# Half of the first expert weights of layer 1 loaded during the attention of its second batch element

## The chip, the cores and the metric

The kernel runs on one core of one Trainium2 chip. A core has a matrix engine (PE, with its weight loads PEld), a vector engine (DVE), a scalar engine (ACT), a general-purpose engine (POOL), and a queue that issues most transfers (SP); 16 DMA engines move the data. All of them run on their own and meet at semaphores. The metric is the device time of one execution in microseconds; lower is better. The whole computation is one launch.

## The reference

Four layers follow each other on an activation `x` of 2 batch elements, 1,024 tokens each, 256 features. Each layer adds a cross-attention over a context of 64 rows and then a second block, each scaled by the tanh of a gate. Layer 1's second block is the one that matters here (NQ = 16 query heads, NKV = 4 key heads, head size 16, 8 experts, HID = 512):

```python
h = rmsnorm(x, ln1_w)
q = rmsnorm(apply_rope(h @ Wq + bq), qn_w)
k = rmsnorm(apply_rope(h @ Wk + bk), kn_w)
v = h @ Wv + bv
...
attn = softmax(where(causal, q k^T / sqrt(HD), -inf))
out = attn v
out = out * sigmoid(out @ Wg + bg)
x = x + out @ Wo + bo
h2 = rmsnorm(x, ln2_w)
logits = h2 @ Wr + br
top1 = argmax(logits)
u = h2 W1[top1] + b1[top1]
act = u[:HID] * sigmoid(u[HID:])
return x + act W2[top1] + b2[top1]
```

Each token goes to one expert. W1 has 256 x 1,024 values for each of the 8 experts, W2 has 512 x 256.

## The kernel before

The 2,048 tokens are 16 tiles of 128 rows. Tiles 0 to 7 are the first batch element, tiles 8 to 15 the second. The self-attention is causal, so a tile attends only to itself and the tiles of its own batch element ahead of it. Memory is given out from two ends: pools on the left, and pools marked `side="right"`, which are held longer. Within PE, layer 1's instructions run in the order in which the program writes them (`manual_schedule`); the other engines' order comes from the framework's scheduler, which also adds waits where a tile takes the memory of an older one.

Stages of layer 1's second block, with what they hold:

- `l1` (L943) opens the right-hand pool `l1f`: 16 row tiles `qk0` to `qk15` (320 values a partition each; rows of q and k, later the new residual `u` in their first 256), `ln2`, the one-hot of the choice `oh`, and the buffer `hbuf` in device memory.
- `l1_front` (L966) makes q, k and v for all 16 tiles, while layer 1's cross-attention still runs. `norm` normalises, `turn` transposes four tiles into `hT` (two buffers), `qkv` multiplies and writes `v` (a tile of 16 x 4 x 32 values, all tokens) and `r` (six buffers), and `divided` turns `r` into the rows `qk`.
- `l1_attention` (L1093) goes tile by tile through the causal attention. `stack` splits a tile's q and k into high and low parts on POOL, and PE transposes them. `greatest` takes scores for the row maxima; their transpose `mT` is copied by DMA, issued by POOL, into the padded rows of `qT` (L1222). `scores` multiplies and exponentiates into `eT` (a pool with three buffers, also named `l1e`); `values` multiplies by `v` into `po`; when a tile is done, its transposes `pq` give `r` and `o` on DVE (L1271, L1273), and the transposes of `o` go into `oT` (a tile of 2 x 2,048 values, all tokens).
- For every group of four finished tiles, `routed` (L1345) queues `gate`, `out` (out-projection, writes the residual `u`), `normed` (writes the normalised rows to `hbuf` by SP, L1321), `turned` and `chosen` (logits and the choice). These are fed one by one between the scores of later tiles: `chosen` of group 1, the first batch element's last, runs while the second element's tiles are being done.
- `l1_experts` (L1564) opens the pool `l1e` with the whole of W1 (`w1`, 2 x 8,192 values a partition, 64 KB) and W2 (`w2`, 8,192 values, 32 KB). SP issues eight loads of W1 of 1 MB each (L1576) and eight of W2 of 1 MB each (L1580). They take memory that attention held, so they start when it is done. `sort_tiles` (L1441) sorts tokens by expert in the pool `l1r`; its constants (a triangular matrix `upper`, five index rows made by POOL iotas at L1427 and copied by DVE at L1429) need no data. Then up to 23 token tiles run, each with one expert: `gather` fetches rows `xg` (L1592) and biases `bt` (L1598) by indices on POOL's queue, `turn` transposes the rows (`xt`, L1609; DVE scales them into `xT`, L1611), `up` multiplies by W1 in two halves of four matmuls (L1625), `back` transposes, `down` multiplies by W2 (`y`, L1645) and scatters the rows to `ybuf`.
- Layer 2 begins with the loads of `l2_l3_xattn` (`lw`, L1815, and `cx`, L1817) and of its weights (`wi`, L1700, and nine further), all on SP, and takes `ybuf` back to `x` in `take` (L1680).

The weights as they were declared and loaded:

```python
w1 = pool.tile([P, DC, E1 * 2 * H1], F32, tag="w1", name="w1")
w2 = pool.tile([P, FC, E1 * D], F32, tag="w2", name="w2")
for e in range(E1):
    nc.sync.dma_start(
        out=w1[:, :, ts(e, 2 * H1)], in_=a["L1_ffn_W1"][e].rearrange("(k p) h -> p k h", p=P)
    )
```

Of the kernel before, what the change touches and what calls it, by code (L numbers as in the profile page):

```python
# [11 lines left out]
F32 = mybir.dt.float32  # L12
# [8 lines left out]
P = 128  # L21
B, S, D = 2, 1024, 256
T = B * S
NT = T // P
# [16 lines left out]
class Net:  # L41
# [901 lines left out]
    def l1(self, take, taken, back):  # L943

        tc = self.tc
        with tc.tile_pool(name="l1f", bufs=1, side="right") as pool:
            rows = [
                pool.tile([P, (NQ + NKV) * HD], F32, tag=f"qk{i}", name=f"qk{i}") for i in range(NT)  # L950
            ]
            ln2 = pool.tile([P, DC], F32, tag="ln2", name="ln2")
            self.nc.sync.dma_start(out=ln2, in_=self.a["L1_ffn_ln2_w"])

            u = [r[:, :D] for r in rows]
            oh = pool.tile([P, NT, E1], F32, tag="oh1", name="oh1")
            hbuf = self.dram.tile([T, D], F32, tag="hbuf", name="hbuf")
            with tc.tile_pool(name="l1a", bufs=1, side="right") as fp:
                es = ExitStack()
                f = self.l1_front(fp, es.enter_context(tc.tile_pool(name="l1q", bufs=1, side="right")), rows)  # L960
                rest = sum(self.l1_xattn(f["steps"], take), [])
                taken()
                self.l1_attention(u, f, rest, es.close, ln2, oh, hbuf)
            return self.l1_experts(ln2, oh, hbuf, back())

    def l1_front(self, keep, pool, rows):  # L966
        nc, a = self.nc, self.a
        NH = NQ + NKV
        n = NH * HD
# [15 lines left out]
        nc.gpsimd.tensor_tensor(kw, kw, kn, ALU.mult)  # L985
        nc.gpsimd.tensor_scalar(kw, kw, HD**-0.5, None, ALU.mult)

        v = keep.tile([P, NT, NKV, 32], F32, tag="v", name="v")
        pv = pool.tile([P, 32], F32, tag="pv", name="pv")
        nc.gpsimd.memset(pv, 0.0)  # L990
        nc.gpsimd.memset(pv[:, HD : HD + 1], 1.0)
# [12 lines left out]
        def padded(i):  # L1004

            kf = kT.rearrange("p h t -> p (h t)")
            if i < 8:
                nc.scalar.copy(kf[64:128, ts(i, 1024)], pk[64:128].to_broadcast([64, 1024]))
            elif i < 10:
                j = slice(8 * (i - 8), 8 * (i - 7))  # L1010
                nc.scalar.copy(
                    v[:, j].rearrange("p i k c -> p (i k) c"),
                    pv[:, None, :].to_broadcast([P, 8 * NKV, 32]),
                )

# [17 lines left out]

        def turn(i):
            if i % 4 == 3:
                hT[i // 4] = pool.tile([P, DC, 512], F32, tag="hT", name="hT", bufs=2)
                self.transposed(
                    [hn[j] for j in range(i - 3, i + 1)], hT[i // 4], 4,
                    evac=lambda o, p, c: nc.scalar.copy(o, p),
                )  # L1040

        def qkv(i):

            p = self.ps("qkv")
# [10 lines left out]
            nc.scalar.copy(  # L1055
                v[:, i, :, :HD], p[:, n:384].rearrange("p (k c) -> p k c", k=NKV)
            )
# [14 lines left out]
            nc.vector.tensor_reduce(group["ss"][:, i % 4, :], sq, AX.X, ALU.add)  # L1072
            nc.vector.tensor_tensor(r, r, t, ALU.add)
# [16 lines left out]
            off=off, ones=ones,  # L1090
        )

    def l1_attention(self, u, front, rest, front_done, ln2, oh, hbuf):  # L1093

# [5 lines left out]
        with ExitStack() as es:  # L1100
# [149 lines left out]
            def values(i, kt, eT):  # L1250
                b, qt = divmod(i, SB)
                if kt == 0:
                    state["po"] = self.psum.tile([P, 512], F32, tag="po", name="po")
                po = state["po"]
                for kv in range(NKV):
                    nc.tensor.matmul(  # L1256
                        po[32 * kv : 32 * kv + 32, :], v[:, b * SB + kt, kv, :], eT[:, kv, :],
                        start=kt == 0, stop=kt == qt,
                    )
                if kt < qt:  # L1260
                    return []
                pT = state["pool"].tile([P, 512], F32, tag="pT", name="pT", bufs=2)
                nc.scalar.copy(pT, po)

                def turn():
                    t = self.ps("pq")
                    for j in range(4):
                        nc.tensor.transpose(t[:, ts(j, P)], pT[:, ts(j, P)], self.ident)
                    t = t.rearrange("p (j k c) -> p k j c", j=4, k=NKV)
                    r = ap.tile([P, NKV, 4], F32, tag="r", name="r", bufs=2)  # L1270
                    nc.vector.reciprocal(r, t[:, :, :, HD])  # L1271
                    o = ap.tile([P, D], F32, tag="o", name="o", bufs=2)
                    nc.vector.tensor_tensor(  # L1273
                        o.rearrange("p (k j c) -> p k j c", k=NKV, j=4), t[:, :, :, :HD],
                        r[:, :, :, None].to_broadcast([P, NKV, 4, HD]), ALU.mult,
                    )
                    state["o"] = o

                def back():
                    t = self.ps("ot")  # L1280
                    for c in range(DC):
                        nc.tensor.transpose(t[:, ts(c, P)], state["o"][:, ts(c, P)], self.ident)
                    nc.scalar.copy(oT[:, :, ts(i, P)], t[:, :D].rearrange("p (c q) -> p c q", c=DC))

                routing.extend(routed(i))
                return [turn, back]
# [2 lines left out]

            def gate(g, c):  # L1290
                p = self.ps("gate")
                o = oT[:, c, ts(g, 512)]
# [5 lines left out]
            def out(i):  # L1298
                p = self.ps("wo")
                nc.tensor.matmul(p[:, :D], ones, borow, start=True, stop=False)  # L1300
                for c in range(DC):
                    nc.tensor.matmul(
                        p[:, :D], oT[:, c, ts(i, P)], wo[:, c, :], start=False, stop=c == DC - 1
                    )

                y = ap.tile([P, D], F32, tag="y", name="y", bufs=2)
# [26 lines left out]
            def chosen(g):  # L1333
# [227 lines left out]
        nc.vector.tensor_copy(sca, row)  # L1561
        return gat, sca, ia

    def l1_experts(self, ln2, oh, hbuf, way):  # L1564
        nc, tc, a = self.nc, self.tc, self.a
        FC = H1 // P
        NS = NT + E1 - 1
# [1 line left out]
        with ExitStack() as es:  # L1569
            pool = es.enter_context(tc.tile_pool(name="l1e", bufs=1, reuse_waits="tile"))  # L1570
            gi, si, ei = (pool.tile([P, NS], I32, tag=n, name=n) for n in ("gi", "si", "ei"))
            used = pool.tile([P, 1], I32, tag="used", name="used")
            w1 = pool.tile([P, DC, E1 * 2 * H1], F32, tag="w1", name="w1")
            w2 = pool.tile([P, FC, E1 * D], F32, tag="w2", name="w2")
            for e in range(E1):
                nc.sync.dma_start(  # L1576
                    out=w1[:, :, ts(e, 2 * H1)], in_=a["L1_ffn_W1"][e].rearrange("(k p) h -> p k h", p=P)
                )
            for e in range(E1):
                nc.sync.dma_start(  # L1580
                    out=w2[:, :, ts(e, D)], in_=a["L1_ffn_W2"][e].rearrange("(k p) d -> p k d", p=P)
# [34 lines left out]
            def up(s, w):  # L1616
# [6 lines left out]
                p, u, h = ups[s], ub[s], slice(w * H1, (w + 1) * H1)  # L1623
                for k in range(DC):
                    nc.tensor.matmul(  # L1625
                        p[:, h], xT[s][:, k, :], w1[:, k, bass.ds(reg[s] * (2 * H1) + w * H1, H1)],
                        start=k == 0, stop=k == DC - 1,
                    )
                nc.vector.tensor_tensor(u[:, h], p[:, h], bt[:, h], ALU.add)  # L1629
# [733 lines left out]
```

## Time and profile before

| | us |
|---|---|
| timed runs | 2134.15, 2143.36, 2151.75 |
| their median | 2143.36 |
| the profiled execution's own time | 2131.65 |
| its span, first to last instruction | 2129.8 |

The profiled execution is one run, a little below the three timed ones; durations below are its own. PE was granted 0.922 of its full clock over the span. Over the span the engines were busy as follows: PE 1832.9 us (86%), PEld 1161.1 (55%), DVE 1130.2 (53%), ACT 839.8 (39%), POOL 416.3 (20%).

The stretches in which layer 1's second block lies, in that execution (times from the start of the span):

| stretch, us | what runs | PE busy | PE clock | GB/s moved |
|---|---|---|---|---|
| 594 to 985 | attention, out-projection, routing | 350.3 of 391 | 0.97 | 6 |
| 985 to 1005 | tail of the routing | 13.0 of 20 | 0.82 | 27 |
| 1005 to 1050 | weights loaded, sort, first token tile | 15.2 of 45 | 0.58 | 358 |
| 1050 to 1165 | the experts | 107.8 of 115 | 1.00 | 120 |
| 1165 to 1185 | change to layer 2 | 6.2 of 20 | 0.66 | 189 |

A busy share is an average over stages with different limits, so a change in one stage is read in that stage. A line of the timeline has the start, the length, the engine, the line of the kernel, the operation, output and inputs, how many instructions were joined (x), and in brackets how long the engine had been idle before and what ended that. The chain of waits goes back from the last instruction to what released each step. A stretch with a DMA share near 1 has all 16 DMA engines taken.

### The profile page before, as it was taken

The page shows a single profiled execution, that of the slowest core. Times are in us where ns is not written, and L with a number is a line of the kernel's source. Part 1 is how long each engine was busy: PE and PEld are TensorE (multiplying, and loading weights), DVE is VectorE, ACT ScalarE, POOL GpSimd, SP SyncE. Part 2 cuts the span into 40 slices and gives each one's busy share as a digit, 9 for nine tenths or more (in the row PEclk, how much of TensorE's full clock was granted, in tenths as well). Part 3 has the DMA queues.
Part 4 walks back from the last instruction along what each step waited for, and adds up shares of the span by engine and source line. Part 5 has one row for each costly group of instructions (what it writes and reads, how often), then busy time and mean ns, then how long its engine had stood idle before and what let it go on. Part 6 is the DMA issues. An engine that isn't in the chain of part 4 may idle for free.

```text
span 2129.8 us, 26730 instructions
## 1 busy us (share of the span) xinstructions
PE 1832.9 (86%) x9860; PEld 1161.1 (55%) x9883; DVE 1130.2 (53%) x2485; ACT 839.8 (39%) x1603; POOL 416.3 (20%) x644
## 2 busy tenths in 40 slices
PE   7858999599778899897598697799999999998894
PEld 3435777466544455544254465455555655656573
DVE  5660100376677737752343776456556555665644
ACT  3402222354534474465011465544444444442131
POOL 1004222111421121023342134100000000000273
PEclk8968999899889999998799896999999999997997
DMA  4033323310000000001742320000000000002135
GB/s 148 21 104 94 116 78 113 90 32 1 7 2 2 1 12 2 2 11 55 291 151 91 104 71 1 1 1 1 1 1 1 1 1 1 1 1 89 38 102 173
DMA packets 70605, 107.12 MB, mean 50 GB/s; under 512 B 13779, under 2 KB 55382, under 8 KB 70214
## 3 DMA queue, kind: packets, MB, share of 16 engines
q1 hardware_dynamic: 54582, 63.17, 9.1%
q0 software_dynamic: 13824, 40.55, 5.7%
q8 instruction: 83, 1.36, 0.3%
q10 hardware_dynamic: 2064, 1.62, 0.2%
q14 instruction: 52, 0.43, 0.1%
HBM read 80.90 MB, written 24.15 MB: 49 GB/s over the span
## 4 chain that ended last, share of the span: by engine, by line
PE 45%; DVE 14%; ACT 7%; issue 6%; POOL 4%; DMA 3%; SPq 1%; ACTq 0%; POOLq 0%; DVEq 0%
PE s L1940 6%; PE et L1962 4%; DVE nm L1947 3%; PE s L1186 3%; PE po L1256 3%; PE sT L1237 3%; PE po L1974 3%; PE h L2130 3%; DVE nm L1192 2%; PE prj L204 2%; ACT e L1949 2%; PE po L352 2%; DMA ybuf<-yo,si 2%; DVE x L236 1%; PE s L554 1%
## 5 line engine op out<-in xcount | busy, mean ns | idle before, releaser
L1949 ACT ACTIVATE e<-s,nm 128x1024 f32<-128x1024 f32 x128 | 141.4, 1110 | 239.7 <-DVE nm L1948 207.6
L1192 DVE TENSOR_REDUCE nm<-s 128x1 f32<-128x512 f32 (+3 forms) x304 | 184.2, 657 | 68.6 <-PE s L1191 46.9
L1947 DVE TENSOR_REDUCE nm<-s 128x1 f32<-128x1024 f32 x128 | 150.4, 1217 | 88.6 <-PE s L1940 88.6
L1245 ACT ACTIVATE eT<-sT 128x512 f32<-128x512 f32 x288 | 148.8, 603 | 112.8 <-PE sT L1237 81.6
L1962 PE MATMUL et<-ident,e 128*128 128x128 f32 x1024 | 143.1, 280 | 22.0 <-ACT qT L219 6.2
L1962 PEld LDWEIGHTS et<-ident,e 128*128 128x128 f32 x1024 | 110.9, 141 | 60.7 <-DVE x L236 11.0
L1186 PE MATMUL s<-kT,qT 128*128 128x512 f32 (+3 forms) x384 | 129.6, 418 | 16.2 <-ACT qT L114 9.7
L1940 PE MATMUL s<-kT,qT 64*128 64x512 f32 x512 | 131.7, 619 | 0.0
L1974 PE MATMUL po<-eT,v 128*64 128x256 f32 x1024 | 124.7, 386 | 0.0
L112 DVE COPY eT<-et 128x512 f32<-128x512 f32 x128 | 87.8, 687 | 58.5 <-PE et L1962 58.3
L1988 POOL TENSOR_TENSOR scs<-scs,nm 128x1024 f32<-128x1024 f32 x8 | 15.2, 1903 | 527.6 <-DVE nm L1948 527.6
L1186 PEld LDWEIGHTS s<-kT,qT 128*128 128x128 f32 x384 | 73.0, 196 | 81.1 <-DVE nm L1192 26.8
L790 PE MATMUL h<-xeT,w 128*128 128x384 f32 (+1 forms) x416 | 109.4, 422 | 0.6 <-DVEq L843 0.3
L800 DVE TENSOR_TENSOR y<-yp,b 128x256 f32<-128x256 f32 (+1 forms) x34 | 14.4, 423 | 177.8 <-PE yp L808 177.2
L794 ACT ACTIVATE hT<-h,b 128x384 f32<-128x384 f32 (+1 forms) x104 | 52.9, 508 | 137.5 <-PE h L790 134.4
L808 PE MATMUL yp<-w,hT 128*128 128x256 f32 x464 | 102.8, 381 | 0.0
L1974 PEld LDWEIGHTS po<-eT,v 128*64 128x64 f32 x1024 | 68.2, 136 | 60.2 <-issue 29.1
L1237 PE MATMUL sT<-qT,kT 128*128 128x512 f32 x288 | 98.0, 455 | 1.8 <-DMA qT<-mT 1.8
L808 PEld LDWEIGHTS yp<-w,hT 128*128 128x128 f32 x464 | 88.0, 190 | 15.3 <-issue 2.1
L114 ACT COPY eT<-et 128x512 f32<-128x512 f32 x128 | 74.0, 592 | 49.5 <-PE et L1962 49.4
L790 PEld LDWEIGHTS h<-xeT,w 128*128 128x128 f32 x416 | 70.8, 192 | 35.6 <-issue 4.0
L1625 PE MATMUL up<-w,xT 128*128 x152 | 77.2, 632 | 14.5 <-DVE ub L1629 7.0
(494 smaller groups left out, 3580.5 us busy)
## 6 DMA issues: line engine op xcount, KB each, us to landing
w<-in_L_ffn_W_dram SPq DMA_DIRECT2D x24, 1024.0 KB, 6.9
y<-ybuf SPq DMA_DIRECT2D x20, 512.0 KB, 5.1
ybuf<-zero POOLq DMA_DIRECT2D x8, 512.0 KB, 7.0
hbuf<-xn SPq DMA_DIRECT2D x32, 128.0 KB, 1.8
w<-in_L_ffn_W_dram SPq DMA_DIRECT2D x8, 512.0 KB, 10.5
x<-in_x_dram SPq DMA_DIRECT2D x16, 128.0 KB, 3.4
hbuf<-hn SPq DMA_DIRECT2D x16, 128.0 KB, 1.7
L_ffn_w1T<-in_L_ffn_w1T_dram SPq DMA_DIRECT2D x1, 2048.0 KB, 7.6
```

The costliest lines, as they stand in the source:

```text
L112: self.nc.vector.tensor_copy(out, in_)
L790: nc.tensor.matmul(p[:, :m], W[e][0][:, k, ts(hc, P)], X[e][:, k, r : r + m], start=k == 0, stop=k == DC - 1,)
L808: nc.tensor.matmul(p[:m, :D], hT[:, hc, r : r + m], W[e][1][:, hc, :], start=hc == 0, stop=hc == HC - 1,)
L1186: nc.tensor.matmul(o, qT[:, h0 + j, :], kT[:, (h0 + j) // 4, b * S + k0 : b * S + k0 + m], start=True, stop=k0 + m < n,)
L1192: nc.vector.tensor_reduce(nm[:, u, h0 : h0 + nh], s[:, : nh * m].rearrange("p (h k) -> p h k", h=nh), AX.X, ALU.max, negate=True,)
L1237: nc.tensor.matmul(s, kT[:, kv, b * S + kt * P : b * S + (kt + 1) * P], qT[:, 4 * kv : 4 * kv + 4, :], start=True, stop=kt < qt,)
L1245: nc.scalar.activation(eT[:, kv, :], s, AF.Exp)
L1940: nc.tensor.matmul(s[h][:, ts(u, 512)], q["qT"][r, 0, ts(t, P)], q["kT"][r, 0, ts(u, 512)], start=True, stop=True,)
L1947: nc.vector.tensor_reduce(m, s[h], AX.X, ALU.max, negate=True)
L1949: nc.scalar.activation(e[n][h], s[h], AF.Exp, bias=m, accum_out=q["rs"][:, t, h : h + 1])
L1962: nc.tensor.transpose(p[:, ts(j, P)], e[n][h][:, ts(k + j, P)], self.ident)
L1974: nc.tensor.matmul(po[j][64 * h : 64 * h + 64, :256], grp[g]["v"][:, k, ts(h, D3X)], eT[j][h][:, k, :], start=k == 0, stop=k == KM - 1,)
```

## The change

One tile `wa` of 8,192 values a partition (32 KB) is opened in the right-hand pool. Until the first batch element is through, it stands in for tiles that had places of their own: `v` and `oT` of the first element (0 to 1,024 and 1,024 to 3,072; the second element has tiles of its own size), the two `hT` buffers of the projections (1,024 to 3,072, ahead of `oT`), the rows `qk0` to `qk7` (3,072 to 5,632) and the ring of six `r` (5,632 to 7,552). When `chosen` of group 1 has been fed, eight loads on SP write the first 128 of the 256 rows of every expert's W1 (0.5 MB each) into `wa`; each waits for what stood in its part. At the start of the experts only the second 128 rows of every W1 are loaded (eight loads of 0.5 MB, in place of the eight of 1 MB), into a tile of half the size; W2 is loaded as before. The up matmuls take their two terms from the two tiles. The number and order of matmuls are as before.

```diff
         with tc.tile_pool(name="l1f", bufs=1, side="right") as pool:
+            wa = pool.tile([P, E1 * 2 * H1], F32, tag="wa", name="wa")
+            n = (NQ + NKV) * HD
             rows = [
-                pool.tile([P, (NQ + NKV) * HD], F32, tag=f"qk{i}", name=f"qk{i}") for i in range(NT)
+                wa[:, 3072 + i * n : 3072 + (i + 1) * n] if i < SB
+                else pool.tile([P, n], F32, tag=f"qk{i}", name=f"qk{i}")
+                for i in range(NT)
             ]
...
-        v = keep.tile([P, NT, NKV, 32], F32, tag="v", name="v")
+        v = [
+            wa[:, 0:1024].rearrange("p (i k c) -> p i k c", k=NKV, c=32),
+            keep.tile([P, SB, NKV, 32], F32, tag="v", name="v"),
+        ]
...
-                hT[i // 4] = pool.tile([P, DC, 512], F32, tag="hT", name="hT", bufs=2)
+                f = 1024 + i // 4 % 2 * 1024
+                hT[i // 4] = wa[:, f : f + 1024].rearrange("p (c t) -> p c t", c=DC)
...
-            r = group[i] = pool.tile([P, NH, HD], F32, tag="r", name="r", bufs=6)
+            f = 5632 + i % 6 * n
+            r = group[i] = wa[:, f : f + n].rearrange("p (h c) -> p h c", c=HD)
...
-            oT = pool.tile([P, DC, T], F32, tag="oT", name="oT")
+            oT = [
+                wa[:, 1024:3072].rearrange("p (c t) -> p c t", c=DC),
+                pool.tile([P, DC, S], F32, tag="oT", name="oT"),
+            ]
...
                 self.first_max(ap, lb, rev, oh[:, 4 * g : 4 * g + 4, :])
+                if g == SB // 4 - 1:
+                    load()
+
+            def load():
+
+                for e in range(E1):
+                    nc.sync.dma_start(out=wa[:, ts(e, 2 * H1)], in_=a["L1_ffn_W1"][e, :P, :])
...
-            w1 = pool.tile([P, DC, E1 * 2 * H1], F32, tag="w1", name="w1")
+            w1 = [wa, pool.tile([P, E1 * 2 * H1], F32, tag="w1", name="w1")]
...
-                nc.sync.dma_start(
-                    out=w1[:, :, ts(e, 2 * H1)], in_=a["L1_ffn_W1"][e].rearrange("(k p) h -> p k h", p=P)
-                )
+                nc.sync.dma_start(out=w1[1][:, ts(e, 2 * H1)], in_=a["L1_ffn_W1"][e, P:, :])
...
-                        p[:, h], xT[s][:, k, :], w1[:, k, bass.ds(reg[s] * (2 * H1) + w * H1, H1)],
+                        p[:, h], xT[s][:, k, :], w1[k][:, bass.ds(reg[s] * (2 * H1) + w * H1, H1)],
```

The other edits index `v` and `oT` by batch element in `values`, `back`, `gate` and `out`, and pass `wa` through `l1`, `l1_front`, `l1_attention` and `l1_experts`.

More of the change, by code (lines that the diff above doesn't have):

```diff
@@ L959, in l1, with l1_front @@
                 es = ExitStack()
-                f = self.l1_front(fp, es.enter_context(tc.tile_pool(name="l1q", bufs=1, side="right")), rows)
+                f = self.l1_front(fp, es.enter_context(tc.tile_pool(name="l1q", bufs=1, side="right")), rows, wa)
                 rest = sum(self.l1_xattn(f["steps"], take), [])
                 taken()
-                self.l1_attention(u, f, rest, es.close, ln2, oh, hbuf)
-            return self.l1_experts(ln2, oh, hbuf, back())
-    def l1_front(self, keep, pool, rows):
+                self.l1_attention(u, f, rest, es.close, ln2, oh, hbuf, wa)
+            return self.l1_experts(ln2, oh, hbuf, wa, back())
+    def l1_front(self, keep, pool, rows, wa):
         nc, a = self.nc, self.a
@@ L1009, in padded @@
             elif i < 10:
-                j = slice(8 * (i - 8), 8 * (i - 7))
                 nc.scalar.copy(
-                    v[:, j].rearrange("p i k c -> p (i k) c"),
+                    v[i - 8].rearrange("p i k c -> p (i k) c"),
                     pv[:, None, :].to_broadcast([P, 8 * NKV, 32]),
@@ L1055, in qkv @@
             nc.scalar.copy(
-                v[:, i, :, :HD], p[:, n:384].rearrange("p (k c) -> p k c", k=NKV)
+                v[i // SB][:, i % SB, :, :HD], p[:, n:384].rearrange("p (k c) -> p k c", k=NKV)
             )
@@ L1091, in l1_front, with l1_attention @@
         )
-    def l1_attention(self, u, front, rest, front_done, ln2, oh, hbuf):
+    def l1_attention(self, u, front, rest, front_done, ln2, oh, hbuf, wa):
         nc, tc, a = self.nc, self.tc, self.a
@@ L1256, in values @@
                     nc.tensor.matmul(
-                        po[32 * kv : 32 * kv + 32, :], v[:, b * SB + kt, kv, :], eT[:, kv, :],
+                        po[32 * kv : 32 * kv + 32, :], v[b][:, kt, kv, :], eT[:, kv, :],
                         start=kt == 0, stop=kt == qt,
@@ L1282, in back @@
                         nc.tensor.transpose(t[:, ts(c, P)], state["o"][:, ts(c, P)], self.ident)
-                    nc.scalar.copy(oT[:, :, ts(i, P)], t[:, :D].rearrange("p (c q) -> p c q", c=DC))
+                    nc.scalar.copy(oT[i // SB][:, :, ts(i % SB, P)], t[:, :D].rearrange("p (c q) -> p c q", c=DC))
                 routing.extend(routed(i))
@@ L1291, in gate @@
                 p = self.ps("gate")
-                o = oT[:, c, ts(g, 512)]
+                o = oT[g // 2][:, c, ts(g % 2, 512)]
                 nc.tensor.matmul(p, wgbd, o, start=True, stop=True)
@@ L1302, in out @@
                     nc.tensor.matmul(
-                        p[:, :D], oT[:, c, ts(i, P)], wo[:, c, :], start=False, stop=c == DC - 1
+                        p[:, :D], oT[i // SB][:, c, ts(i % SB, P)], wo[:, c, :], start=False, stop=c == DC - 1
                     )
@@ L1562, in place, with l1_experts @@
         return gat, sca, ia
-    def l1_experts(self, ln2, oh, hbuf, way):
+    def l1_experts(self, ln2, oh, hbuf, wa, way):
         nc, tc, a = self.nc, self.tc, self.a
```

## The prediction

> **What bounds the kernel now.** The page says PE, 86% busy. An edit that moves weight loads is decided where PE is not busy, so I went from the table by stretches (five microseconds each) to the one place where the DMA engines are full, the start of layer 1's experts. Columns: stretch, length, busy time and count of PE, PEld, DVE, ACT, POOL; then granted clock, DMA share, GB/s.
> ```profile
> 995.00:1005.00 10.00, 6.16 (x24) 4.98 (x24) 0.62 (x4) 1.36 (x4) 8.59 (x14) 0.65 0.16 53
> 1010.00:1015.00 5.00, 0.00 (x0) 0.00 (x0) 5.00 (x25) 0.00 (x0) 0.00 (x0) 0.50 1.02 416
> 1035.00:1040.00 5.00, 4.22 (x6) 1.34 (x5) 0.69 (x1) 1.91 (x2) 0.00 (x0) 0.50 1.06 365
> 1045.00:1050.00 5.00, 2.20 (x6) 0.96 (x6) 1.75 (x4) 0.99 (x2) 0.94 (x1) 1.00 0.78 245
> 1060.00:1080.00 20.00, 18.96 (x71) 11.27 (x70) 8.24 (x16) 3.34 (x6) 9.70 (x10) 1.00 0.40 138
> ```
> From 1008 to 1048 us all DMA engines are taken, at 350 to 416 GB/s, and PE does little. The chain of waits there (start, length, what) shows which transfer ends last: a W2 load, L1580, behind SP's queue. The timeline below it (start, length, engine, line, instruction, in brackets the idle time before it and what ended it) shows what PE does at both waits:
> ```profile
> 1015.35 4.76 SPq L1580
> ...
> 1039.89 10.18 DMA w<-in_L_ffn_W_dram
> 1050.07 0.45 issue
> 1050.52 1.97 PE y L1645 x8
> ```
> ```profile
> 1005.27 6.38 SPq L1576 DMA_DIRECT2D w<-in_L_ffn_W_dram  x8
> 1025.59 0.66 PE L1609 MATMUL xt<-ident,xg 128*128 128x128 f32 x2 [8.89 <-DMA xg<-hbuf,gi]
> 1026.29 0.42 DVE L1611 TENSOR_TENSOR xT<-xt,ln 128x256 f32<-128x256 f32 x1 [7.87 <-PE xt L1609]
> 1032.98 3.75 PE L1625 MATMUL up<-w,xT 128*128 x4 [6.73 <-DMA w<-in_L_ffn_W_dram]
> 1037.52 3.78 PE L1625 MATMUL up<-w,xT 128*128 x4 [0.78 <-DVE ub L1629]
> 1047.01 0.38 PE L1609 MATMUL xt<-ident,xg 128*128 128x128 f32 x2
> 1050.52 1.97 PE L1645 MATMUL y<-w,aT 128*128 x8 [3.13 <-DMA w<-in_L_ffn_W_dram]
> ```
> Eight W1 loads (L1576, 1 MB each) are issued from 1005.27, eight W2 loads (L1580) behind them; in the program each W2 load waits on SP for the W1 load eight places before it, so W2 trails W1. PE has its first token tile ready at 1026.7 (0.42 after 1026.29) and waits for W1 until 1032.98, then for W2 from 1047.39 to 1050.52. Later PE is 95% busy. The layer before those loads (attention, to 985 us) leaves the DMA engines empty: 1 to 23 GB/s in the 25-us stretches.
>
> **The change, part by part.**
> *W1's first halves leave the burst.* 8 x 0.524 = 4.19 MB less. Moved between 1005 and 1050, from the stretches (238, 416, 411, 406, 406, 390, 365, 348, 245 GB/s for 5 us each): 16.1 MB; 12.6 are weights, the rest gathers. After: W1's second halves, 4.19 MB, reach that sum at about 1017, and at 1029 if W2 and gathers take half of every microsecond; wanted at 1026.7. I take 1017: W2 trails W1. So up starts 0.05 after xT (as the later tiles do): 1026.8 instead of 1032.98, 6.2 us. It cannot start sooner unless the gather lands sooner.
> *W2's wait.* Wanted 3.13 earlier for its own wait and 6.2 for the shift: 1041.2. Until then W1's halves, W2 and five tiles' rows and four tiles' biases (0.13 and 0.66 MB each) are 11.7 MB, which the old rates reach at about 1036. The wait of 3.1 goes, with 5 us to spare. Next late is PE itself.
> *The first gather.* It lands 6.2 us after issue inside the burst, against a median of 2.9. The burst is still there at 1019 (W2), so I take no gain; bounds 0 and 3.3.
> *Clock.* PE's up groups run at 0.50 until 1041, some 8 us after PE starts at 1032.98, then eight matmuls of 593 ns take half as long. PE will be idle from 1006 to 1025 still, so I move the cold stretch with it, at no gain or loss; bounds: one group of four cold or warm, 3.78 against 1.98, 1.8 either way. The Trainium skill (TensorE: Matmul & The Clock Gate, Part 1, What's actually happening) says that one busy window of about 3.4 us releases the clock. By that rule the second group would run warm and the sum be 1.8 better; the trace's 8 us disagrees, so the measurement stands.
> *The early loads.* SP issues eight loads of 0.5 MB at 0.5 us each (the W1 issues' median 493 ns); nobody waits for SP there. By the built program, parts 6 and 7 go when the projections' last normalised rows are out (DVE, 594 and 604), part 3 with the first group's residual (777), part 0 after the eighth tile's last values (811), parts 1 and 2 after the out-projection (916), 4 and 5 after the second group's residual (924, 926). Queued behind each on SP are the hbuf writes (770, 919, 966, 997), whose rows are not made before the loads ahead of them are freed. A load moves in 1.3 us (0.524 MB at 0.405). Cost 0; bounds below under the slower rival.
> *The tiles placed in wa.* The same instructions in the same order on PE, ACT and DVE through the attention; the residual's DVE write gains a wait on POOL's split of the same row, over 100 us earlier. Cost 0.
> *The sort's constants.* Less memory moves them onto the exponentials' buffers, so the built program puts POOL's memset and five iotas, before at 604, behind the last pq transposes, and five DVE copies around the last o:
> ```profile
> 604.38 0.20 POOL masks.py:65 MEMSET upper<- 128x128 f32 x1
> 604.54 0.16 POOL L1427 IOTA iai<- 128x23 int32 x1
> ...
> 984.12 0.26 DVE L1271 RECIPROCAL r<-pq 128x16 f32<-128x16 f32 x1 [7.15 <-PE pq L1268]
> 984.41 0.42 DVE L1273 TENSOR_TENSOR o<-pq,r 128x256 f32<-128x256 f32 x1
> ```
> Behind the DVE copy ia, which waits for the first iota, stand o, then PE's ot and the whole routing tail. 984.12 + 0.20 + 0.16, a hand-over near 0.1 and a copy of 0.17 end at 984.75 against 984.41: 0.3 lost; upper bound all six POOL steps (1.07) and five copies (0.85): 1.9. POOL is next wanted at 995.27.
> *Into layer 2.* SP's lw and cx now wait only for up's last matmul, not for the last scatter:
> ```profile
> 1169.60 0.34 SPq L1815 DMA_DIRECT2D lw<-in_L_xattn_ln_dram  x1
> 1170.77 0.38 SPq L1700 DMA_DIRECT2D wi<-in_L_ffn_weight_qT_dram  x1
> ```
> wi and the nine issues behind it can start at lw's old place, 1.17 earlier; the last of them that counts, bk, takes 4.34 us from 1174.30 to its landing in the chain of waits, and DVE's next step follows it. I take 1.0, bounds 0 and 1.2.
>
> **Sum:** 6.2 + 3.1 + 1.0 - 0.3 = 10.0 us. The profiled execution took 2131.65 (span 2129.8, 1.85 around it) and would take 2121.7. It is the fastest of four; the three timed runs are 2134.15, 2143.36, 2151.75, and the four average 2140.2. A median of new runs I put at 2140.2 - 10.0 = 2130.
>
> **Rivals.**
> *Smaller loads move slower, W2 still ends last.* For it: the only half-megabyte loads of the burst, W2's, are in flight where the rate sinks to 348 and 245; against: there the queue also runs dry. At 300 GB/s 11.7 MB take 39 us from 1006, so W2 comes at 1045 instead of 1050.52: 5.5 + 0.7 = 6.2 gained, 2134. The Trainium skill (DMA: Bandwidth & Descriptors, Bandwidth, Measured) has 341 GB/s for 1 MB and asks for at least 1 MB a transfer; by it the halves would be slower, and this trace's 1-MB loads, eight at once, moved 406 to 416.
> *The early loads are not early* (a region held to the end): no gain, 2140. Against it: the waits named above, all met by 926.
> *Slower: the early loads hold up the rows that attention needs.* POOL's mT copies into qT use the same DMA engines, and PE's scores wait for them:
> ```profile
> DMA to landing us min/median/max: 1.7/1.7/3.3
> ```
> One of 32 made PE wait, 1.8 us, at 612. Eight loads, each costing such a landing of 3.3, are 26 us: net 16 slower, 2156; it decides from the fourth stall on. Against it: copies meet loads only near 777, 811 and 924, and later tiles' copies are made a whole tile, 8 us or more, ahead of their scores.
>
> **Numbers.** Forecast 0.80, slow loads 0.09, not early 0.04, stalls 0.04, anything else 0.03. Steps range from 6.2 - 0.3 - 1.8 to 10.3 + 1.2 + 3.3 + 1.8 - 0, so 4 to 16 us of gain; timed runs of one kernel spread by 18 us, a median of them by some 6 either way. 2140 less 16 and less 4, and 6 at the ends partly: 2119 to 2142, which takes in the slow-loads and not-early cases. A change below 1% can hardly be told from none here: 10 us is 0.47%. Faster by over 1% needs 21 us, so the scatter: 0.09. Within 1%: 0.87. Slower: 0.04, the stalls and part of the rest.
>
> **What would show it.** Right: no DMA wait in front of the first up (near 1027) nor the first y (near 1041), W1 halves landed before 1020, early loads all issued by 926, o some 0.3 later after its reciprocal, the gap before layer 2 a microsecond shorter. Wrong: PE's waits in attention for qT growing, a DMA wait left at the first y, a cold stretch longer than 8 us, or the first gather becoming later than 1025.

## The result, and the profile after

The changed kernel takes 2132.72 us, the kernel before 2143.0 us (medians of 16 runs each): 10.3 us less. The ratio of the two sets of runs is 0.9955, that is 9.6 us less, with a 95% interval of 0.994 to 0.9969, between 6.6 and 12.9 us. The forecast was 10.0 us less and 2130 us.

The two profiled executions, 2129.8 us before and 2127.8 us after, differ by only 2.0 us, and that pair is misleading. After layer 1 nothing was changed, and yet the last stage of layer 3 (from its first row write to its first read back) took 165.4 us in the one and 182.0 us in the other. All experiments below show one of these two lengths: 182 to 187 in e1_place, e2_w2twice, e3_const and e6_twice, which ran together on one chip, and 161 to 165 in the other five, which ran on two others. The short one was traced with the new and the old placement alike; the long one was traced with the new placement only, but the timed runs of the kernel before were some 21 us longer on that chip as well (2144.14 against 2123.19 and 2120.88). So it does not go with the change, and what the change did is read in the stretch that it touches, between two marks of the same profile. From the first write of normalised rows to `hbuf` to DVE's first step of layer 2 (L236, the residual added) it was 414.8 us before (770.30 to 1185.12) and is 405.7 us after (761.84 to 1167.58): 9.1 us less.

Where these went, stage by stage. First the table by five-microsecond stretches of the changed kernel, with the columns of the prediction (the last three: granted clock, DMA share, GB/s):

```profile
1000.00:1005.00 5.00, 0.00 (x0) 0.00 (x0) 4.86 (x29) 0.00 (x0) 0.00 (x0) 0.50 1.00 406
1010.00:1015.00 5.00, 0.00 (x0) 0.00 (x0) 0.75 (x6) 0.00 (x0) 2.74 (x3) 0.50 1.10 350
1020.00:1025.00 5.00, 4.22 (x6) 1.51 (x5) 0.69 (x1) 1.36 (x2) 2.22 (x3) 0.50 1.03 385
1025.00:1030.00 5.00, 4.10 (x9) 1.53 (x8) 1.62 (x3) 0.56 (x1) 0.95 (x1) 0.79 1.06 371
1030.00:1035.00 5.00, 4.65 (x21) 2.94 (x19) 2.31 (x4) 1.11 (x2) 0.95 (x1) 1.00 0.06 19
```

The DMA engines are full from 1000 to 1030, 30 us instead of 43, and PE works in the last twelve of them. Its timeline in the changed kernel shows what became of the two waits:

```profile
1017.84 0.66 PE L1628 MATMUL xt<-ident,xg 128*128 128x128 f32 x2 [8.72 <-DMA xg<-hbuf,gi]
1019.08 2.04 PE L1644 MATMUL up<-wa,xT 128*128 x2 [0.57 <-DVE xT L1630]
1020.91 1.92 PE L1644 MATMUL up<-w,xT 128*128 x2
1023.61 2.08 PE L1644 MATMUL up<-wa,xT 128*128 x2 [0.78 <-issue]
1028.45 1.13 PE L1644 MATMUL up<-wa,xT 128*128 x2 [0.90 <-DVE xT L1630]
...
1033.04 0.38 PE L1628 MATMUL xt<-ident,xg 128*128 128x128 f32 x2
1033.25 1.89 PE L1664 MATMUL y<-w,aT 128*128 x8
```

The first up group follows its xT, 1.24 us after the start of xt, where it was 7.39 before. The first y follows the matmul ahead of it with no wait. SP's timeline has the early loads (L1364) and what stands between them:

```profile
585.24 10.21 SPq L1364 DMA_DIRECT2D wa<-in_L_ffn_W_dram  x2
...
768.61 139.58 SPq L1364 DMA_DIRECT2D wa<-in_L_ffn_W_dram  x4
911.60 2.03 SPq L1335 DMA_DIRECT2D hbuf<-hn  x4
917.69 1.02 SPq L1364 DMA_DIRECT2D wa<-in_L_ffn_W_dram  x2
958.32 33.48 SPq L1335 DMA_DIRECT2D hbuf<-hn  x8
997.71 3.87 SPq L1597 DMA_DIRECT2D w<-in_L_ffn_W_dram  x8
1001.82 13.15 SPq L1599 DMA_DIRECT2D w<-in_L_ffn_W_dram  x8
```

(A line joins issues of one kind; its length runs from the first to the last.) All eight are out by 918.7, at the times that the prediction gives less 6 to 9 us, by which this profile is earlier; which of the eight parts each carries, the timeline does not say. The first two go at 585, although the program has them behind `chosen` of group 1.

### The profile page after: what moved, and what is told of

It is laid out like the page before. It is cut to its first block, busy times and chain, and to the rows that moved or that the text cites. A ratio compares the mean times of both kernels' runs of the same rounds, so it can differ in the third digit from the quotient of the medians.

```text
span 2127.8 us, 26776 instructions
## 1 busy us (share of the span) xinstructions
PE 1824.8 (86%) x9883; PEld 1155.4 (54%) x9883; DVE 1129.0 (53%) x2485; ACT 839.5 (39%) x1603; POOL 417.3 (20%) x644
## 4 chain that ended last, share of the span: by engine, by line
PE 45%; DVE 14%; ACT 7%; issue 6%; POOL 5%; DMA 3%; ACTq 0%; SPq 0%; another core or an unknown queue 0%; POOLq 0%; DVEq 0%
PE s L1959 6%; PE et L1981 4%; PE s L1200 3%; PE po L1270 3%; DVE nm L1966 3%; PE po L1993 3%; PE sT L1251 3%; PE h L2149 2%; DVE nm L1206 2%; PE prj L204 2%; ACT e L1968 2%; PE po L352 2%; DMA ybuf<-yo,si 2%; DVE x L236 1%; PE s L554 1%
## 5 line engine op out<-in xcount | busy, mean ns | idle before, releaser
L1428 POOL DMA_INDIRECT ybuf<-yo,si x58 | 57.3, 988 | 75.5 <-DVE yo L1669 38.2
```

## The experiments

Each experiment's ratio is to runs of the kernel before on the same chip, 12 runs against 23 to 35. An interval is some 0.2% to either side, 4 us, so differences of 1 to 3 us are read from the traces. One table for all of them, in us; the wait is PE's at the first y, the last column runs from the last tile's pq transposes to layer 2's first step on DVE:

| kernel | ratio (interval) | first hbuf write to last pq | pq to o | first xt to first up | first up to first y | wait for W2 | last y to layer 2 | last pq to layer 2 |
|---|---|---|---|---|---|---|---|---|
| before | 1 | 213.1 | 0.99 | 7.39 | 17.54 | 3.13 | 22.20 | 201.7 |
| changed | 0.9955 (0.994, 0.9969) | 213.9 | 1.23 | 1.24 | 14.17 | 0 | 22.00 | 191.8 |
| e1_place | 0.9996 (0.9978, 1.0014) | 213.1 | 1.22 | 6.68 | 18.30 | 2.89 | 21.95 | 201.2 |
| e1b_halves | 0.9996 (0.9974, 1.0018) | 211.0 | 0.98 | 7.05 | 18.21 | 2.81 | 22.31 | 203.5 |
| e2_w2twice | 1.0022 (1.0001, 1.0043) | 214.5 | 1.23 | 1.18 | 25.82 | 11.39 | 21.50 | 204.6 |
| e3_const | 0.9968 (0.9951, 0.9986) | 213.9 | 0.98 | 1.17 | 14.27 | 0 | 21.06 | 191.2 |
| e4_hold | 0.9982 (0.9959, 1.0005) | 214.4 | 1.22 | 1.17 | 23.15 | 8.72 | 21.25 | 199.8 |
| e5_warm | 0.9955 (0.9935, 0.9975) | 215.5 | 1.22 | 1.08 | 13.28 | 2.47 | 21.53 | 192.2 |
| e6_twice | 0.9966 (0.9948, 0.9985) | 214.8 | 1.22 | 1.33 | 13.32 | 0.93 | 21.90 | 192.2 |
| e7_best | 0.9958 (0.9941, 0.9976) | 215.3 | 0.99 | 1.08 | 11.56 | 0.75 | 21.64 | 189.1 |
| e8_bt3 | 0.9972 (0.9954, 0.9991) | 214.2 | 1.22 | 1.17 | 12.27 | 0 | 21.75 | 190.8 |

**Placement without the early loads (e1_place).** The shared tile stays, its loads go when attention is done. Their place in the program alone would not hold them back, because a load is issued as soon as its memory is free (as the two at 585 were), so they are tied to POOL's last step of attention.

```diff
-                if g == SB // 4 - 1:
-                    load()
...
-                    nc.gpsimd.tensor_tensor(self.x[i], self.x[i], u[i], ALU.add)
+                    self.last = nc.gpsimd.tensor_tensor(self.x[i], self.x[i], u[i], ALU.add).ins
...
             for e in range(E1):
+                self.after(
+                    nc.sync.dma_start(out=wa[:, ts(e, 2 * H1)], in_=a["L1_ffn_W1"][e, :P, :]), [self.last]
+                )
                 nc.sync.dma_start(out=w1[1][:, ts(e, 2 * H1)], in_=a["L1_ffn_W1"][e, P:, :])
```

> The tiles stand in the shared tile as in the changed kernel, but both halves of W1 are loaded when attention is done, sixteen loads of 0.5 MB in pairs by expert, W2 behind them. Theory (the gain comes from the 4.19 MB that leave the burst): the burst is 43 us long again, the first up matmul waits about 6 us for W1 and the first y about 3 us for W2, and the time is that of the kernel before, ratio 0.999 to 1.002 (the later constants cost 0.7 us, nothing else changes). Rival 1 (the new placement itself gains, by freeing memory or by other waits): ratio near 0.9955 with both waits back. Rival 2 (loads of 0.5 MB move slower than those of 1 MB): the burst moves at some 300 GB/s instead of 350 to 416, W2's wait grows by 5 us or more and the ratio is 1.002 to 1.005.

PE's timeline in this kernel:

```profile
1021.45 2.05 PE L1645 MATMUL up<-wa,xT 128*128 x2 [6.02 <-DMA wa<-in_L_ffn_W_dram]
1024.16 2.04 PE L1645 MATMUL up<-w,xT 128*128 x2 [0.66 <-DMA w<-in_L_ffn_W_dram]
...
1039.75 1.97 PE L1665 MATMUL y<-w,aT 128*128 x8 [2.89 <-DMA w<-in_L_ffn_W_dram]
```

Both waits are back (6.02 + 0.66, where the kernel before had 6.73, and 2.89, where it had 3.13), and so is the time. The gain is the early loads', not the placement's. Rivals 1 and 2 fall.

**Half-size loads in the old kernel (e1b_halves).**

```diff
-                nc.sync.dma_start(
-                    out=w1[:, :, ts(e, 2 * H1)], in_=a["L1_ffn_W1"][e].rearrange("(k p) h -> p k h", p=P)
-                )
+                for k in range(DC):
+                    nc.sync.dma_start(out=w1[:, k, ts(e, 2 * H1)], in_=a["L1_ffn_W1"][e, ts(k, P), :])
```

> The kernel before with each W1 load of 1 MB issued as two of 0.5 MB, nothing else changed. Theory (at 350 to 416 GB/s with eight loads in flight the size does not matter): the waits of the kernel before, some 6.5 us at the first up and 3 us at the first y, ratio 0.998 to 1.002; the constants are made early and o starts 1.0 us after the first of its pq transposes. Rival (smaller loads move slower, as the Trainium skill has it in DMA: Bandwidth & Descriptors, Bandwidth, which asks for 1 MiB or more): the burst is 3 to 13 us longer, ratio 1.001 to 1.006.

PE's timeline in this kernel:

```profile
1019.35 2.04 PE L1624 MATMUL up<-w,xT 128*128 x2 [6.38 <-DMA w<-in_L_ffn_W_dram]
1022.30 2.05 PE L1624 MATMUL up<-w,xT 128*128 x2 [0.91 <-DMA w<-in_L_ffn_W_dram]
```

The waits are 6.38 + 0.91 us there and 2.81 at the first y, the ratio 0.9996. With eight loads in flight, W1's 0.5 MB moves like its 1 MB: in e1_place the full stretches ahead of the first up ran at 399 to 412 GB/s, before at 406 to 416. So the size of a load does not slow it here, and the prediction's rival of slower halves falls. The Trainium skill's advice of 1 MiB or more a transfer (DMA: Bandwidth & Descriptors, Bandwidth) did not show in this burst; its table is of transfers issued from GpSimd, and these go on SP's queue, eight at a time.

**The bytes put back behind W1 (e2_w2twice).**

```diff
-            for e in range(E1):
+            for e in list(range(E1)) * 2:
                 nc.sync.dma_start(
                     out=w2[:, :, ts(e, D)], in_=a["L1_ffn_W2"][e].rearrange("(k p) d -> p k d", p=P)
                 )
```

> The changed kernel with every W2 load issued twice, which puts 4.19 MB, the bytes that left the burst, back into it behind W1's halves. Theory (W2 has only a few microseconds to spare, the full stretch ended at 1030 and y wanted W2 at 1033.2): W1's wait stays gone, the first y waits for W2 by 10.4 us (4.19 MB at 0.405 MB per us) less the 3 to 5 us to spare, 5.5 to 7.5 us, and two thirds of the gain are lost: ratio 0.998 to 0.9995. Rival (W2 is early by a wide margin, as W2 was last only because it queued behind whole W1 loads): no wait at y, ratio 0.9955 as the changed kernel.

First its timeline of PE at the first y, then its stretches:

```profile
1040.52 0.38 PE L1628 MATMUL xt<-ident,xg 128*128 128x128 f32 x2
1052.29 3.58 PE L1664 MATMUL y<-w,aT 128*128 x8 [11.39 <-DMA w<-in_L_ffn_W_dram]
```

```profile
1040.00:1045.00 5.00, 0.90 (x4) 0.28 (x2) 1.62 (x3) 0.00 (x0) 0.94 (x1) 1.00 1.09 348
1045.00:1050.00 5.00, 0.00 (x0) 0.00 (x0) 0.00 (x0) 0.00 (x0) 0.00 (x0) 0.53 1.08 344
1050.00:1055.00 5.00, 2.71 (x7) 2.20 (x8) 0.00 (x0) 0.00 (x0) 0.00 (x0) 0.50 0.03 11
```

The wait moved to y and is larger than expected, 11.39 us; the idle time then cost the clock as well (y's eight matmuls 3.58 us instead of 1.89). W1's wait stayed gone and the kernel was no faster than before: **taking away the first wait alone is worth nothing.** What pays is that 4.19 MB fewer stand ahead of the last W2 load. From the last pq to layer 2 e2_w2twice is even 2.9 us slower than the kernel before (204.6 against 201.7); 1.6 of these are the first y at the lower clock. The miss of 4 us is in the rate and in the spare time: the added bytes moved at 344 to 348 GB/s, which is the rate of W2's loads by themselves (below, under W2's wait), 12.1 us instead of 10.4, and little was spare. How little, the kernels below in which y waits tell: W2 was in, and y began, 14.36 us after the first xt in e5_warm and 14.65 in e6_twice. In the changed kernel y comes 15.41 us after it, so W2 has about 1 us to spare: 12.1 - 1 = 11.1, near the 11.39.

**The early loads twice (e6_twice).**

```diff
-                for e in range(E1):
+                for e in [e for e in range(E1) for n in range(2)]:
                     nc.sync.dma_start(out=wa[:, ts(e, 2 * H1)], in_=a["L1_ffn_W1"][e, :P, :])
```

> The changed kernel with every early load issued twice, 8.4 MB instead of 4.19 MB moved during attention. Theory (attention leaves the DMA engines nearly empty and nobody waits for these loads): attention takes as long as in the changed kernel, from the first hbuf write to the last pq within 1 us, ratio 0.9945 to 0.9965. Rival (the early loads hold up POOL's copies into qT, which PE waits for): PE's wait for qT grows by 1.8 us or more for each copy met, attention longer by 2 us or more against the changed kernel, and that kernel pays half of this already: ratio 0.997 or more.

The table of PE's waits from 760 to 985 us (what waited, for what; total, times, longest) has one such line in the changed kernel and one in this one, where the kernel before has none in that stretch:

```profile
PE sT L1251 <- DMA qT<-mT: 0.6, 1, 0.6
```

```profile
PE sT L1251 <- DMA qT<-mT: 1.3, 1, 1.3
```

The rival's mechanism exists. In the changed kernel SP issues one early load at 802.21 and POOL the copies of mT at 802.23, and the scores that need them wait 0.6 us. It is one collision, not eight of 3.3: each of the seven profiles with the eight early loads has one such wait in this stretch, of 0.6 to 0.9 us, the one with sixteen has one of 1.3, and the three without early loads have none. Attention from the first hbuf write to the last pq is 0.8 us longer in the changed kernel than before and 1.7 longer here, but the kernels with the same loads scatter there from 213.9 to 215.5, and the two with the old placement lie 2.1 apart, so only the waits are firm. No copy cost anything like 1.8 us or more, and the ratio does not tell the cases apart.

**The constants early (e3_const).** The triangular matrix and the five index rows get memory of their own in the right-hand pool.

```diff
+            upper = pool.tile([P, P], F32, tag="upper", name="upper")
+            make_upper_triangular(self.nc, upper, 1.0, diag=False)
+            ns = NT + E1 - 1
+            made = dict(
+                upper=upper, ia=self.iota(pool, ns, tag="ia"), ib=self.iota(pool, P, tag="ib"),
...
         nc = self.nc
+        if tag in self.made:
+            return self.made[tag]
```

> The changed kernel with the sort's five index rows and its triangular matrix made early, from memory of their own, so that they no longer wait for the exponentials' buffers. Theory (the constants hold up the last o by 0.7 us: o starts 1.3 us after its pq transposes instead of 0.6): o starts 0.6 us after the last pq again, the routing tail is 0.7 us earlier, ratio 0.9952 where the changed kernel has 0.9955, too little to tell in the time. Rival (o waits for something else, the copies having only filled its wait): o still starts 1.3 us after pq.

o starts 0.98 us after pq, as before the change, 0.25 us sooner than in the changed kernel. The cause in that kernel is in DVE's timeline:

```profile
976.44 0.26 DVE L1285 RECIPROCAL r<-pq 128x16 f32<-128x16 f32 x1 [7.15 <-PE pq L1282]
976.89 0.20 DVE L1450 CAST ia<-iai 128x23 f32<-128x23 int32 x1 [0.18 <-POOL iai L1448]
976.98 0.42 DVE L1287 TENSOR_TENSOR o<-pq,r 128x256 f32<-128x256 f32 x1
```

The copy ia stands ahead of o and waits for POOL's iota. The expectation's 0.7 us was too high: it compared o with different matmuls of the last pq group in the two profiles. The rival falls.

**W2 held for the first gather (e4_hold).** W2's loads are issued after the first gather and made to wait for its landing.

```diff
+            def rest():
+                for e in range(E1):
+                    self.after(
+                        nc.sync.dma_start(
+                            out=w2[:, :, ts(e, D)], in_=a["L1_ffn_W2"][e].rearrange("(k p) d -> p k d", p=P)
+                        ),
+                        [got[0].ins],
+                    )
...
                 for s in range(a, min(a + 2, b)):
                     G[s] = gather(s)
+                    if s == 0:
+                        rest()
```

> The changed kernel with the W2 loads held on SP until the first gather has landed; W1's halves go as before. Theory (the first gather is slowed by the W2 loads in flight, and the bytes set when W2 is in): the gather lands 3 us after its issue instead of 6.1, xT and the first up matmul are 3 us earlier, but the DMA engines then idle some 4 us, and W2 with the later gathers (some 8 MB at 0.36 MB per us from 1014.5) is in near 1036 of the changed kernel's time against y's want at 1030: y waits some 6 us, the net is 3 us slower than the changed kernel, ratio 0.9965 to 0.9975. Rival (W2 has time to spare): no wait at y, 3 us faster than the changed kernel, ratio 0.994.

The gather and what depends on it were 3.2 us sooner (2.99 us from POOL's issue to xt, against 6.19), and y, in PE's timeline of this kernel, paid for it:

```profile
1017.61 0.66 PE L1634 MATMUL xt<-ident,xg 128*128 128x128 f32 x2 [5.52 <-DMA xg<-hbuf,gi]
...
1041.93 3.75 PE L1670 MATMUL y<-w,aT 128*128 x8 [8.72 <-DMA w<-in_L_ffn_W_dram]
```

The net is 8 us slower than the changed kernel (199.8 against 191.8): 3 were expected. The wait at y was 8.72 where some 6 were expected, and while PE waited its clock fell (0.50 from 1040 to 1045), so that the time from the first y to the last became 3.0 us longer (115.3 against 112.3). The burst's order as it stands, W2 ahead of the gathers, is the better of the two.

**PE warmed (e5_warm), and with fewer bias buffers and early constants (e7_best); the buffers alone (e8_bt3).**

```diff
             with tc.manual_schedule(engines={mybir.EngineType.PE}):
+                t = self.ps("idle")
+                for j in range(7):
+                    nc.tensor.matmul(
+                        t, self.ident, self.ctxT.rearrange("p c b j l -> p (c b j l)"), start=True, stop=True
+                    )
                 tiles(0, most)
```

```diff
-                bt = pool.tile([P, 2 * H1 + D], F32, tag="bt", name="bt", bufs=4)
+                bt = pool.tile([P, 2 * H1 + D], F32, tag="bt", name="bt", bufs=3)
```

> The changed kernel with seven matmuls of a constant by the identity (128 by 512, output read by nobody) on PE between the sort's last matmuls and the first token tile, where PE idles 8.7 us for the first gather. Theory (PE's clock is let up by some 8 us of PE work, as the trace shows, and falls back in idle time): the seven take some 7 us at half clock, the first up group then runs at least partly at full clock, two cold groups of 3.75 us become 2.0 us each: 1.8 to 3.6 us earlier at the second tile, ratio 0.9938 to 0.9947 where the changed kernel has 0.9955. By the Trainium skill (TensorE: Matmul & The Clock Gate, Part 1, What's actually happening: about 3.4 us of a busy window) both groups run warm. Rival 1 (what is gained there is lost at y, since W2 now lands last): the first y waits for W2 by 1 to 3 us, ratio as the changed kernel. Rival 2 (the clock does not follow PE's own work): both groups stay at 3.75 us.

> The changed kernel with the constants early, the seven warming matmuls, and three buffers instead of four for the gathered biases, so that one gather of 0.66 MB leaves the time in which W2 moves. Theory (with PE warm, the first y is late by 2.5 us because W2 shares the DMA engines with the gathers): 0.66 MB at 0.36 MB per us is 1.8 us, so the wait for W2 falls from 2.5 to about 0.7 us; with 0.24 us from the constants the stretch from the last pq to layer 2's first step is some 189 us against 191.8, ratio 0.9940 to 0.9948. Rival (fewer bias buffers make PE wait for a bias later): the steady tiles become longer, y to last y over 112.4 us by more than 1 us, and the ratio is 0.9955 or more.

> The changed kernel with three buffers instead of four for the gathered biases alone. Theory (in the changed kernel nothing waits for W2, so bytes taken from the burst bring nothing more): first y and everything after it as in the changed kernel within 0.5 us, ratio 0.9945 to 0.9965. Rival (the gathers still slow the first tiles there): first y 1 us or more earlier after the first up.

In e5_warm the PE stretches of half a microsecond (PE busy and count, granted clock, DMA share, GB/s), then its timeline:

```profile
1020.50:1021.00 0.50, 0.50 (x2) 0.50 1.11 356
1021.00:1021.50 0.50, 0.50 (x2) 0.85 1.09 348
1021.50:1022.00 0.50, 0.50 (x2) 1.00 1.19 365
```

```profile
1018.48 7.57 PE L1697 MATMUL idle<-ctxT,ident 128*128 128x512 f32 x14
...
1028.88 1.10 PE L1644 MATMUL up<-wa,xT 128*128 x2 [0.67 <-DVE xT L1630]
...
1031.62 1.13 PE L1644 MATMUL up<-wa,xT 128*128 x2 [0.78 <-DVE ub L1648]
...
1042.16 1.97 PE L1664 MATMUL y<-w,aT 128*128 x8 [2.47 <-DMA w<-in_L_ffn_W_dram]
```

Both up groups run warm, the third group starts 5.83 us after the first instead of 9.37, and 2.47 of the 3.5 us are lost again at y: now W2 is late, as its rival 1 said, and the ratio is the changed kernel's. The 1 us that is left does not show in the last column, because another stage scatters by as much: from the last o to the sort's first matmul it took 22.3 to 22.6 us in e5_warm, e6_twice and e8_bt3 and 21.2 to 21.3 in the other eight profiles. None of the three edits is in that stage; the cause stays open. In e7_best one bias gather fewer goes beside W2 and y waits 0.75 us, as expected; the stretch from the last pq to layer 2 is 189.1 us, 2.7 less than in the changed kernel, while its ratio 0.9958, above the 0.9940 to 0.9948 that were expected, cannot be told from 0.9955. In e8_bt3 y came 1.9 us sooner after the first up than in the changed kernel, where the theory allowed 0.5, as its rival said, but not by the rival's cause. Its PE timeline:

```profile
1021.06 1.71 PE L1644 MATMUL up<-w,xT 128*128 x2
1023.55 1.12 PE L1644 MATMUL up<-wa,xT 128*128 x2 [0.78 <-DVE ub L1648]
```

The second group is warm here without any warming, and so it is in e6_twice; in the changed kernel the same group took 2.08 us for its first pair. With four bias buffers, in e6_twice, y then waits 0.93 us for W2; with three, in e8_bt3, it does not wait. So, as far as this pair shows, the buffers pay only where PE is early.

## Why the prediction was right, and where its steps were off

**W1's wait.** Forecast 6.2 us, measured 6.15 (xt to up, 7.39 to 1.24); e1_place shows it returns with the late loads. W1's halves were in before the gather, which stayed at 6.2 us as forecast (6.19 from POOL's issue to xt), and e4_hold measured the upper bound given for it, 3.3, as 3.2.

**W2's wait.** Forecast 3.1, measured 3.37 (up to y, 17.54 to 14.17): the wait of 3.13 and some 0.2 of PE. The term held, and its cover was mis-sized: "with 5 us to spare" is about 1 us. The step that was off is the 11.7 MB "at the old rates". The amount is right (from 1000 to 1030 the stretches add to 11.5 MB), but the old rates until 1030, 406 to 416 GB/s, were those of W1's loads and of gathers (none of W2's smaller packets moved from 1010 to 1030), and W2's loads move slower by themselves. The first three lines below are of the changed kernel: from 1000 to 1006 us W1's halves move, from 1010 to 1016 W2, and the third line is the only queue of that second stretch, SP's, so no gather has moved yet. The last line is W2 alone in the kernel before, from 1038 to 1046:

```profile
DMA packets 674, 2.45 MB, mean 408 GB/s; under 512 B 76, under 2 KB 76, under 8 KB 674
DMA packets 2112, 2.10 MB, mean 350 GB/s; under 512 B 64, under 2 KB 2112, under 8 KB 2112
q1 hardware_dynamic: 2112, 2.10, 109.5%
DMA packets 2782, 2.78 MB, mean 348 GB/s; under 512 B 79, under 2 KB 2781, under 8 KB 2781
```

(The counts of packets by size include all smaller ones.) Both kinds of load are of 0.5 MB here: W2 has 512 x 256 values of 4 bytes for an expert, 0.5 MB and not the 1 MB that the section on the kernel before gives for its loads. W1's rows of 1,024 values go in packets of 4 KB, W2's rows of 256 values in packets of 1 KB. That is the difference which the view shows; it was not varied by itself. So the prediction's rival had read rightly that the rate sinks to 348 where W2's loads are in flight, and the answer given to it, "there the queue also runs dry", does not hold: the DMA engines were full then (share 1.10 from 1040 to 1045). The gathers do not lower the total, 371 to 385 GB/s from 1015 to 1030, but W2 gets little of it: from 1017 to 1028 SP's queue moved 1.08 of 4.22 MB. Of the some 4 us that are missing, 1.6 are these rates (11.7 MB are reached at 1030 and not at 1028.4, the prediction's 1036 less the 7.6 us by which the loads now begin earlier), 1.3 a thin end (SP's last packet ends at 1031.27), and 0.9 the way from that packet to y (in e2_w2twice the last packet ends at 1051.35 and y begins at 1052.29). It did not decide the time, but e2_w2twice, e4_hold and e5_warm show that it does as soon as W2 is later or PE sooner.

**Constants.** Forecast 0.3 lost, measured 0.24, by the mechanism that was named (ia waits for the iota, o stands behind it).

**Into layer 2.** Forecast 1.0 gained. From the last y to DVE's first step it was 22.20 and 22.31 us in the two kernels with the old placement, and 22.00 in the changed kernel; over the nine profiles with the shared tile it is 21.06 to 22.00, 21.6 in the mean, so some 0.6. lw and cx do go ahead of the last scatter's landing now, but wi goes 4.05 to 5.53 us after POOL issued that scatter, where lw's old place was 3.95 after it. The forecast gave wi that place exactly. The scatter itself lands later: 2.40 us after its issue in the two kernels with the old placement, 3.12 to 3.22 in e4_hold, e5_warm, e7_best and e8_bt3, the four shared-tile profiles that show its landing, and the load that waits for it follows 1.5 us later in all six. That lw and cx, now moving beside it, hold it up fits this and was not tried by itself.

**The early loads.** Forecast 0, measured 0.6 lost as a wait and 0.8 in the length of the attention: one collision with the copies of mT at the place named for it ("near 777, 811 and 924" in the old profile's time; 802 here is the 811). The slower rival named the right mechanism and priced it at eight times 3.3.

**The sum.** 6.15 + 3.37 + 0.2 - 0.24 - 0.8 = 8.7 from these five stages in the one pair of profiles, 9.1 with the rest between the two marks (0.3 of it between the last o and the first xt), against a forecast of 10.0 and 10.3 us timed with an interval of 6.6 to 12.9. The too high transition and the uncounted collision, 1.6 us together, lie within what the timing can resolve, so the timed agreement to 0.3 us is partly luck.

**The clock.** The prediction set the Trainium skill's window (TensorE: Matmul & The Clock Gate, Part 1, What's actually happening) aside because PE's work stayed cold for 8 us. The cold stretch did move along, as forecast, but that reason was wrong. In e5_warm PE works without a break from 1017.86 and the clock is let up in the stretch at 1021.0, after some 3.3 us. The 8 us are two groups of 3.75 us with a break of 0.78 us. The traces' records of the granted clock show steps: the stretch at 0.50 around these groups lasts 44.37 us in the kernel before, 37.55 in the changed kernel, 34.13 in e6_twice and e8_bt3 and 23.89 in e5_warm and e7_best, each a whole number of times 3.41 us. The same page says in that section that its window of 3.4 us runs free and does not start with the work; in that reading, a group of 3.75 us fills nearly a whole window only by chance, and the profiles agree: the second group is cold before and after the change and warm in e6_twice and e8_bt3. In these two the clock comes up 3.17 and 3.24 us after the start of the first group; in the changed kernel the steps, counted back from 1027.14, fall at 1020.31 and 1023.73, so that the break of 0.78 us lies inside one. The either-way 1.8 us of the range was therefore the right size for it.

## What to carry to other kernels

When two waits stand behind one queue of transfers, the earlier one is worth nothing by itself: ask when the last load of the queue is in, and count everything that moves beside it, gathers on other queues too, each at the rate that it shows where it moves alone. Moving bytes into a stage with idle DMA engines is nearly free, and the price to look for is the odd small copy that PE waits for there. A change of half a per cent is read between two marks inside the trace, since an unchanged stage elsewhere can differ by more than the change between two executions.

## What the hardware showed unexpectedly

An unchanged stage of layer 3 took 161 to 165 us in some executions and 182 to 187 in others; kernels that ran together agreed, whatever their code. The long ones among the experiments ran on one chip and the short ones on two others, so chip and time of running are not told apart, and the cause stays open. Loads of the same 0.5 MB on the same queue moved at 408 GB/s in packets of 4 KB and at 350 in packets of 1 KB. And the clock of PE came up inside the first group of cold up matmuls in two of the profiles and only near the end of the second or later in others with the same order of instructions, which moved the first y by 0.9 to 1.9 us.
